# A windowed-attention and Fourier-mixing kernel: image 1 loaded ahead of the mode weights, image transposes in pairs of rows, the group norm without matmuls, and another order where there is no feed-forward and in the tail

## Chip, cores and metric

The kernel runs on one core of one Trainium2 chip. The metric is the device time of one execution in microseconds; lower is better. All data are 32-bit floats.

## What is computed

The input is 32 images of 56 x 56 tokens with 128 channels. There are two layers, each with a residual:

```python
def _gn(v, G=32, eps=1e-5):            # group norm: 32 groups of 4 channels, over the whole image
    g = v.reshape(B_, H_, W_, G, C_ // G)
    m = jnp.mean(g, axis=(1, 2, 4), keepdims=True)
    s = jnp.var(g, axis=(1, 2, 4), keepdims=True)
    return ((g - m) / jnp.sqrt(s + eps)).reshape(v.shape)
...
# layer 0: attention in windows of 7 x 7 tokens, 4 heads, image rolled by 3 in both directions
qkv = (win @ w_qkv.T).reshape(-1, N, 3, NH, hd)
attn = softmax(q @ k^T * scale + bias[rel_idx] + shift_mask)
out = (attn @ v) @ w_proj.T + b_proj   # rolled back
# layer 1: Fourier mixing along both axes, then a feed-forward
out_y = jnp.einsum('bixy,ioy->boxy', dct(x)[..., :32], w0)    # 32 modes, along the width
xy = idct(out_y padded with zeros)
...                                                           # the same along the height with w1
h = relu((xx + xy) @ W1 + b1) @ W2 + b2
# the network
x = x + layer0(_gn(x))
x = x + layer1(_gn(x))
```

## The kernel before

**Tiling.** An image is cut into 8 rows of 8 windows (a row is 7 image lines, 392 tokens). The work is a software pipeline over cycles: cycle r starts row r of all 256 (`row(cycle)` gives the image and the row; i = cycle mod 8 is the row in the image). Rows of one image are followed by those of the next without a break. The order in which TensorE (PE), ScalarE (ACT), VectorE (DVE) and GpSimd (POOL) get their instructions is written out by hand: it is the order in which the Python functions are called. Transfers are issued by the SP queue, in that order too.

**The attention of a row** goes through several cycles. In its own cycle: `attn_qk` (queries and keys, L321 and L328; VectorE writes one half of the keys, L341), `attn_v` (L353), `attn_scores` (L375, then two additions of the bias on VectorE, L383), `attn_max` (L393, and a subtraction on POOL, L394), `attn_exp` (L400). A cycle later `attn_divide` (sum L405, reciprocal L407, product on POOL, L408). Two cycles later `attn_transpose` (L419), `attn_values` (L444, evacuated to oT on ACT at L477 and on VectorE at L475), and `attn_project` (L486), whose sum with the image (L494) is written to a scratch tensor in HBM (L500). `attn_sums` (L508, L517) takes the sums for the second group norm.

**The Fourier layer of an image** starts ten cycles after its first row; c counts its cycles, so c = 0 falls on i = 2. c = 0: statistics (L528, L537) and the transform along the width (L595); c = 1, 2: that along the height, from columns loaded out of the scratch tensor; c = 3 to 5: the mode mixing (`mix`, L629), written to HBM (L639); c = 4 to 7: loaded again (`load_modes`, L650) and transformed back (`modes_back`, L668). The feed-forward of seven token groups is at c = 7, 8, 9, 10, 12, 13, 14 (`FF_AT`): `ff_in` (L711, with relu on ACT, L719; the residual is loaded at L694 and gets b2 on POOL, L701) and `ff_out` (L731, addition on VectorE L740, output DMAs L752, L753, L760). Since c goes past 8, a cycle holds the end of one image's Fourier layer and the start of the next one's. Only at c = 3 and c = 11, both on i = 5, there is no feed-forward.

**A cycle** is `full_first` (transposes, queries and keys, `load_modes`, `ff_in`, ...), then `quarters` (scores and `modes_back`), `half_columns` (`attn_v`, `transform`, `mix`), `eighths` (values), and `full_last` (`ff_out`, the next image's transposes, exponential, projection). The first ten cycles, where there is no Fourier work, are written in `first_rows`. After the last row the same functions run on with what is left of the last image.

**The next image.** `next_image` issues its load at i = 2 (L114; two buffers, so the load waits until the buffer's former image is transformed, L595) and calls `image_group` for its rows at i = 4 (2 rows), 5 (3) and 6 (3). Each call transposes four chunks of 112 tokens (two image lines each; L259), though a row is 3.5 chunks; ACT copies the row's 392 columns out of PSUM (L269), VectorE takes bn_stats (L270), POOL adds the projection's bias to the image (L274). `image_norm` is a generator, and the calls of `next(norm)` place its parts: bn_aggr (L281) at the end of i = 6; in i = 7 a matmul with the group-averaging matrix (L284), four small VectorE operations, a second such matmul (L297), the power -0.5 on POOL (L301), L303, the scaling of the qkv weights on ACT (L308) and a third matmul (L310).

**PSUM.** Four banks ("pa") rotate through all attention and image work, four ("pc") through the rest. A matmul that takes a bank waits for the readers of its last use, four allocations earlier.

**Before the cycles** the constants are loaded: image 0, small ones, the bias table (L182 adds it up on VectorE), then the mode weights w1sb and w0sb of 2 MB each and those of the feed-forward (all L125). Image 1 is loaded by `next_image` in cycle 2, so behind them in SP's queue.

## Time and profile before

| | |
|---|---|
| median of 9 runs | 3696.25 us (3694.11 to 3698.69) |
| profiled execution, its time | 3694.72 us |
| profiled execution, span from first to last instruction | 3692.9 us |
| mean granted TensorE clock | 0.997 |
| TensorE matmuls busy | 3626.5 us |
| TensorE weight loads busy | 2964.4 us |
| VectorE / ScalarE / GpSimd busy | 2183.5 / 2149.7 / 1372.3 us |
| image transposes (L259), instructions and busy | 1024, 129.9 us |
| norm matmuls L284 and L297, busy | 9.3 and 12.4 us |

A line of the timeline has the start in us from the span's start, the time from the first start to the last end of a block of equal instructions, engine, line, operation, the tiles written and read, shapes and count; in brackets stands the idle time ahead of it and what ended it. A matmul of 32-bit data is two instructions, a transpose one. Matmuls are pipelined, so that a printed block overlaps the next one. A line of the waits has the waiting instruction, what it waited for, the sum in us, how often, and the longest.

### The profile page before, as it was taken

What the parts mean: (1) busy time and instruction counts of PE and PEld (TensorE: products, weight loads), DVE (VectorE), ACT (ScalarE), POOL (GpSimd) and SP (SyncE); (2) the same over time, 40 slices, a digit from 0 to 9 for tenths busy, and PEclk for the clock granted to TensorE, in tenths of its full rate; (3) what the DMA queues carried; (4) which work ended last, traced back from release to release, by engine and by line L of the source; (5) the groups of instructions that cost most, each with busy time, mean ns of one, the idle gap of its engine ahead of it and who ended that gap; (6) DMA issues with size and microseconds to landing.
All of it is one profiled execution on the core that took longest, in us unless ns stands there. A gap on an engine that the chain in (4) does not pass through costs nothing.

```text
span 3692.9 us, 139935 instructions
## 1 busy us (share of the span) xinstructions
PE 3626.5 (98%) x61440; PEld 2964.4 (80%) x61440; DVE 2183.5 (59%) x4577; ACT 2149.7 (58%) x3915; POOL 1372.3 (37%) x1421
## 2 busy tenths in 40 slices
PE   6899999999999999999999999999999999999998
PEld 5678888888888888888888888878888888888786
DVE  6655665565666556655656665566655566565641
ACT  4555565555656555665556566556665565565653
POOL 5333343433333333434333343334333333433321
PEclk9999999999999999999999999999999999999999
DMA  4333434343434334343434343343344343443332
GB/s 112 97 99 105 114 91 111 106 112 101 113 93 116 105 103 116 92 110 105 112 101 113 95 114 107 105 113 97 105 109 109 102 113 97 111 107 105 96 107 89
DMA packets 687778, 388.93 MB, mean 105 GB/s; under 512 B 40480, under 2 KB 658113, under 8 KB 686913
## 3 DMA queue, kind: packets, MB, share of 16 engines
q1 hardware_dynamic: 686557, 379.65, 37.6%
q8 instruction: 484, 7.93, 0.9%
q14 instruction: 126, 1.02, 0.1%
q10 hardware_dynamic: 611, 0.32, 0.0%
HBM read 218.29 MB, written 161.48 MB: 103 GB/s over the span
## 4 chain that ended last, share of the span: by engine, by line
PE 93%; DVE 4%; DMA 1%; SPq 1%; ACT 1%; issue 0%; POOL 0%; ACTq 0%; POOLq 0%; DVEq 0%
PE pc L731 20%; PE pc L711 18%; PE pa L353 7%; PE pc L629 6%; PE pc L595 6%; PE pa L375 6%; PE pa L419 5%; PE pa L486 5%; PE pc L668 5%; PE pa L328 5%; PE pa L444 4%; PE pa L321 4%; PE pa L259 2%; DVE st L270 1%; DVE a L383 1%; DVE mx L393 1%
## 5 line engine op out<-in xcount | busy, mean ns | idle before, releaser
L408 POOL TENSOR_TENSOR a<-a,rs 128x784 f32<-128x784 f32 x256 | 389.9, 1523 | 1230.8 <-DVE rs L407 965.0
L731 PE MATMUL pc<-wff,hid 128*128 128x128 f32 (+1 forms) x6400 | 778.4, 279 | 0.9 <-ACT hid L719 0.7
L731 PEld LDWEIGHTS pc<-wff,hid 128*128 128x128 f32 (+1 forms) x6400 | 731.0, 189 | 21.0 <-issue 1.9
L711 PE MATMUL pc<-xf,wff 128*128 128x512 f32 (+2 forms) x1792 | 713.1, 540 | 0.4 <-ACT z L637 0.4
L719 ACT ACTIVATE hid<-pc,b1sb 128x512 f32<-128x512 f32 (+2 forms) x896 | 536.6, 635 | 97.6 <-PE pc L711 93.9
L711 PEld LDWEIGHTS pc<-xf,wff 128*128 128x128 f32 x1792 | 337.0, 190 | 301.1 <-issue 229.5
L394 POOL TENSOR_TENSOR a<-a,mx 128x784 f32<-128x784 f32 x256 | 389.5, 1522 | 451.6 <-DVE mx L393 451.2
L740 DVE TENSOR_TENSOR res<-pc,res 128x512 f32<-128x512 f32 (+2 forms) x256 | 143.6, 571 | 597.2 <-issue 273.7
L427 ACT COPY aT<-pa 113x452 f32<-113x452 f32 x256 | 137.7, 538 | 457.8 <-PE pa L419 457.7
L274 POOL TENSOR_TENSOR xl<-xl,bproj 112x384 f32<-112x384 f32 (+1 forms) x256 | 291.9, 1142 | 247.7 <-PE pa L259 243.4
L383 DVE TENSOR_TENSOR a<-pa,bm 128x392 f32<-128x392 f32 x512 | 259.5, 549 | 199.5 <-PE pa L375 199.3
L341 DVE TENSOR_SCALAR k<-pa,heads,bqkv 128x392 f32<-128x392 f32 x246 | 168.5, 685 | 275.1 <-ACT k L333 275.1
L475 DVE TENSOR_SCALAR oT<-pa,bqkv 128x98 f32<-128x98 f32 (+2 forms) x768 | 170.7, 278 | 267.7 <-PE pa L444 267.7
L400 ACT ACTIVATE a<-a 128x784 f32<-128x784 f32 x256 | 222.8, 870 | 169.9 <-POOL a L394 169.6
L360 ACT COPY v<-pa 128x512 f32<-128x512 f32 x256 | 152.6, 596 | 276.3 <-PE pa L353 276.3
L701 POOL TENSOR_TENSOR res<-res,b2sb 128x512 f32<-128x512 f32 (+2 forms) x256 | 263.6, 1036 | 100.3 <-DMA res<-scr 83.7
L375 PEld LDWEIGHTS pa<-k,q 64*64 64x64 f32 x8192 | 183.3, 132 | 137.8 <-DVE rs L407 68.2
L353 PE MATMUL pa<-wn,xw 128*64 128x128 f32 x4096 | 281.4, 280 | 3.6 <-DVE a L383 3.5
L353 PEld LDWEIGHTS pa<-wn,xw 128*64 128x64 f32 x4096 | 219.3, 137 | 51.4 <-issue 17.0
L393 DVE TENSOR_REDUCE mx<-a 128x16 f32<-128x784 f32 x256 | 247.2, 966 | 5.7
L419 PE MATMUL pa<-ident,a 113*113 113x113 f32 x2048 | 248.3, 264 | 1.6 <-POOL a L408 1.6
L405 DVE TENSOR_REDUCE sm<-a 128x16 f32<-128x784 f32 x256 | 245.7, 960 | 5.1 <-ACT a L400 5.1
(89 smaller groups left out, 5890.1 us busy)
## 6 DMA issues: line engine op xcount, KB each, us to landing
zscr<-z SPq DMA_DIRECT2D x512, 112.0 KB
htok<-scr SPq DMA_DIRECT2D x256, 196.0 KB
zT<-zscr SPq DMA_DIRECT2D x192, 256.0 KB
res<-scr SPq DMA_DIRECT2D x160, 256.0 KB
out_dram<-res SPq DMA_DIRECT2D x128, 256.0 KB
scr<-xl SPq DMA_DIRECT2D x128, 224.0 KB
xl<-in_x_dram SPq DMA_DIRECT2D x32, 784.0 KB
xl<-in_x_dram SPq DMA_DIRECT2D x32, 672.0 KB
```

Of the source, the lines that this page charges most:

```text
L274: nc.gpsimd.tensor_tensor(piece, piece, bproj.unsqueeze(1).to_broadcast([TC, n1 - n0, C]), ALU.add)
L353: nc.tensor.matmul(pv[hs, j * C : (j + 1) * C], lhsT=im.xw[i][:, w * WT : w * WT + JP], rhs=im.w[:, 2 * C : 3 * C], start=True, stop=True,)
L375: nc.tensor.matmul(ps[hp][HALVES[e], pr * 2 * WT : (pr + 1) * 2 * WT], lhsT=q[cs, w * WT : w * WT + JP], rhs=k_sb[cs, :, w], start=True, s ...
L383: nc.vector.tensor_tensor(a[:, 2 * hp : 2 * hp + 2, :, 0:WT].rearrange("p u w j -> p w u j"), ps[hp][:, :RT].rearrange("p (w u j) -> p w u ...
L393: nc.vector.tensor_reduce(mx, a3, axis=AX.X, op=ALU.max)
L394: nc.gpsimd.tensor_tensor(a3, a3, mx.unsqueeze(2).to_broadcast([P, 2 * NWR, WT]), ALU.subtract)
L408: nc.gpsimd.tensor_tensor(a3, a3, rs.unsqueeze(2).to_broadcast([P, 2 * NWR, WT]), ALU.mult)
L419: nc.tensor.transpose(pt[:PW, h * P : h * P + PW], a[:PW, h, 2 * hf : 2 * hf + 2].rearrange("p w j -> p (w j)")[:, :PW], ident[:PW, :PW],)
L701: nc.gpsimd.tensor_tensor(res[:m, c0:c1], res[:m, c0:c1], b2sb[:m].unsqueeze(1).to_broadcast([m, c1 - c0, C]), ALU.add,)
L711: nc.tensor.matmul(ph[:, :n], lhsT=wff1[:, f * P : (f + 1) * P], rhs=xff[:, t0 : t0 + n], start=True, stop=True,)
L719: nc.scalar.activation(hf[:, :n], ph[:, :n], AF.Relu, bias=b1sb[:, f : f + 1])
L731: nc.tensor.matmul(pf[:m, c * C : (c + 1) * C], lhsT=im.hid[f][:, c * P : c * P + m], rhs=wff2[:, f], start=(f == 0), stop=(f == NF - 1),)
```

## The change

1. Image 1 is loaded before the mode weights instead of in cycle 2.
2. `image_group` becomes `image_groups`: two rows at once out of seven transposes in two PSUM banks, at i = 3, 4, 5 and 6. ACT copies the first row in one piece and the second in two.
3. `image_norm` averages over the groups on VectorE: the statistics are transposed in blocks of 32, reduced over four, broadcast, and transposed back. The two matmuls with the averaging matrix go, and the whole calculation up to the power is in the first part of i = 7.
4. Cycles without a feed-forward put `half_columns` ahead of `quarters`. Before, the rule was c = 3; now it also holds for the first image's cycles c = 0, 1, 2, 4, 5, 6, where no earlier image has a feed-forward to do.
5. In the tail, after the last row's attention, the order is `half_columns`, `ff_out`, `quarters`; before it was `quarters`, `half_columns`, `ff_out`. The very last output group is added and written chunk by chunk.

```diff
--- before.py
+++ after.py
@@ -205,6 +205,8 @@
             nc.sync.dma_start(idcth[ls, : S - SS], src[:, SS:])
             nc.sync.dma_start(idcth[ls, S - SS :], src[:, :SS])
     idcth = idcth.rearrange("p h r -> p (h r)")
+    if NB > 1:
+        xls[1] = load_image(1)
     w1sb = const_load([P, NM, C], w1, "w1sb")
     w0sb = const_load([P, NM, C], w0, "w0sb")
     wff1 = const_load([P, FF], W1, "wff1")
@@ -249,63 +251,99 @@
         im.scr = dram.tile([S, S, C], F32, tag="scr", name="scr", bufs=2)
         return im
-    def image_group(im, i):
-        pt = attn_bank()
-        pt4 = pt[:, : 8 * S].rearrange("p (j r s) -> p j r s", r=8, s=WS)
-        for c in range(4):
+    def image_groups(im, i):
+        pt = [attn_bank(), attn_bank()]
+        pts = [
+            p[:, : n * S].rearrange("p (j r s) -> p j r s", r=n, s=WS) for p, n in zip(pt, (8, 6))
+        ]
+        for c in range(7):
             nc.tensor.transpose(
-                pt4[:, :, 2 * c : 2 * c + 2],
+                pts[c // 4][:, :, 2 * (c % 4) : 2 * (c % 4) + 2],
                 im.x[:, WS * i // 2 + c],
                 ident_x[:, :, SS:].rearrange("p r (j s) -> p j r s", s=WS),
             )
-        mine = pt4[:, :, i % 2 : i % 2 + WS].rearrange("p j r s -> p j (r s)")
-        im.xw[i] = big.tile([P, RT + JP - WT], F32, tag="xw", name="xw", bufs=10)
-        nc.gpsimd.memset(im.xw[i][:, RT:], 0.0)
-        xw = im.xw[i][:, :RT]
-        nc.scalar.copy(xw.rearrange("p (j t) -> p j t", t=WT), mine)
-        nc.vector.bn_stats(im.st[:, i], xw)
-        n0, n1 = WS * i // 2, WS * (i + 1) // 2
-        piece = im.x[:, n0:n1]
-        nc.gpsimd.tensor_tensor(
-            piece, piece, bproj.unsqueeze(1).to_broadcast([TC, n1 - n0, C]), ALU.add
-        )
+        for k in range(2):
+            im.xw[i + k] = big.tile([P, RT + JP - WT], F32, tag="xw", name="xw", bufs=10)
+            nc.gpsimd.memset(im.xw[i + k][:, RT:], 0.0)
+            xw = im.xw[i + k][:, :RT]
+            dst = xw.rearrange("p (j r s) -> p j r s", r=WS, s=WS)
+            if k:
+                nc.scalar.copy(dst[:, :, 0], pts[0][:, :, WS])
+                nc.scalar.copy(
+                    dst[:, :, 1:].rearrange("p j r s -> p j (r s)"),
+                    pts[1].rearrange("p j r s -> p j (r s)"),
+                )
+            else:
+                nc.scalar.copy(
+                    dst.rearrange("p j r s -> p j (r s)"),
+                    pts[0][:, :, :WS].rearrange("p j r s -> p j (r s)"),
+                )
+            nc.vector.bn_stats(im.st[:, i + k], xw)
+        n0, n1 = WS * i // 2, WS * (i + 2) // 2
+        for a, e in ((n0, n0 + 4), (n0 + 4, n1)):
+            piece = im.x[:, a:e]
+            nc.gpsimd.tensor_tensor(
+                piece, piece, bproj.unsqueeze(1).to_broadcast([TC, e - a, C]), ALU.add
+            )
+    stat = const.tile([P, C // 4], F32, tag="stat", name="stat")
+    nc.vector.memset(stat, 0.0)
     def image_norm(im):
-        mv = small.tile([P, 2], F32, tag="mv", name="mv")
-        nc.vector.bn_aggr(mv, im.st)
+        GR = C // 16
+        def average(out, src):
+            sums = small.tile([P, GR], F32, tag="gsums", name="gsums", bufs=2)
+            nc.vector.tensor_reduce(
+                sums, src.rearrange("p (g c) -> p g c", c=4), axis=AX.X, op=ALU.add
+            )
+            nc.vector.tensor_scalar(
+                out.rearrange("p (g c) -> p g c", c=4),
+                sums.unsqueeze(2).to_broadcast([P, GR, 4]),
+                0.25,
+                None,
+                ALU.mult,
+            )
         yield
-        pg = attn_bank()
-        nc.tensor.matmul(pg[:, 0:1], lhsT=gavg, rhs=mv[:, 0:1], start=True, stop=True)
-        gm = small.tile([P, 1], F32, tag="gm", name="gm")
-        nc.vector.tensor_copy(gm, pg[:, 0:1])
+        nc.vector.bn_aggr(stat[:, 0:2], im.st)
+        turned = small.tile([P, 32], F32, tag="turned", name="turned", bufs=2)
+        nc.vector.transpose(turned, stat)
+        mean = small.tile([P, 2, 32], F32, tag="gmeans", name="gmeans", bufs=2)
+        average(mean[:, 0], turned)
+        nc.vector.tensor_tensor(turned, turned, mean[:, 0], ALU.subtract)
+        nc.vector.tensor_tensor(turned, turned, turned, ALU.mult)
+        average(mean[:, 1], turned)
+        back = small.tile([P, 2, 32], F32, tag="back", name="back", bufs=2)
+        nc.vector.transpose(
+            back.rearrange("p k c -> p (k c)"), mean.rearrange("p k c -> p (k c)")
+        )
+        gm = back[:, 0, 0:1]
         nc.vector.tensor_scalar(im.xw[0][:, RT : RT + 1], gm, -1.0, None, ALU.mult)
-        d = small.tile([P, 1], F32, tag="d", name="d")
-        nc.vector.tensor_tensor(d, mv[:, 0:1], gm, ALU.subtract)
-        e = small.tile([P, 1], F32, tag="e", name="e")
+        ve = small.tile([P, 1], F32, tag="ve", name="ve")
         nc.vector.scalar_tensor_tensor(
-            out=e, in0=d, scalar=d, in1=mv[:, 1:2], op0=ALU.mult, op1=ALU.add
-        )
-        yield
-        pv = attn_bank()
-        nc.tensor.matmul(pv[:, 0:1], lhsT=gavg, rhs=e, start=True, stop=True)
-        ve = small.tile([P, 1], F32, tag="ve", name="ve")
-        nc.vector.tensor_scalar(ve, pv[:, 0:1], 1e-5, None, ALU.add)
+            out=ve, in0=back[:, 0, 1:2], scalar=1e-5, in1=back[:, 1, 0:1], op0=ALU.add, op1=ALU.add
+        )
         rstd = small.tile([P, 1], F32, tag="rstd0", name="rstd0")
         nc.gpsimd.tensor_tensor(rstd, ve, mhalf, ALU.pow)
+        im.w = work.tile([P, 3 * C], F32, tag="wn", name="wn")
+        yield
         nb = small.tile([P, 1], F32, tag="nb0", name="nb0")
         nc.vector.scalar_tensor_tensor(
             out=nb, in0=gm, scalar=-1.0, in1=rstd, op0=ALU.mult, op1=ALU.mult
         )
-        im.w = work.tile([P, 3 * C], F32, tag="wn", name="wn")
+        nc.scalar.mul(im.w, wqkv, rstd)
         yield
-        nc.scalar.mul(im.w, wqkv, rstd)
         pb = attn_bank()
         nc.tensor.matmul(pb[:, 0:1], lhsT=wqkv[:, 2 * C :], rhs=nb, start=True, stop=True)
         im.bias = small.tile([P, 5], F32, tag="bqkv", name="bqkv")
@@ -735,7 +773,10 @@
                     start=(f == 0),
                     stop=(f == NF - 1),
                 )
-        for c0, c1, m in ((0, k, P), (k, k + 1, last)):
+        parts = [(0, k, P), (k, k + 1, last)]
+        if im.b == NB - 1 and g == len(FF_GROUPS) - 1:
+            parts = [(c, c + 1, m) for c, m in enumerate(chunks)]
+        for c0, c1, m in parts:
             if m:
                 nc.vector.tensor_tensor(
                     res[:m, c0:c1],
@@ -754,7 +795,7 @@
                 c += 1
                 continue
             e = c + 1
-            while e < len(chunks) and chunks[e] == m and (o >= NT or o + (e + 1 - c) * m <= NT):
+            while len(parts) == 2 and e < len(chunks) and chunks[e] == m and (o >= NT or o + (e + 1 - c) * m <= NT):
                 e += 1
             o %= NT
             nc.sync.dma_start(
@@ -850,11 +891,15 @@
         if im:
             attn_values(im, i, cycle - 2)
-    def full_last(cycle, norm):
-        next(norm)
+    def last_out(cycle):
         for im, c in fourier(cycle):
             if c in FF_AT:
                 ff_out(im, FF_AT.index(c))
+    def full_last(cycle, norm):
+        next(norm)
+        if row(cycle - 2)[0]:
+            last_out(cycle)
         next_image(cycle)
         if row(cycle)[0]:
             attn_exp(cycle)
@@ -868,8 +913,8 @@
         if b + 1 < NB:
             if i == 2:
                 images[b + 1] = image_begin(b + 1)
-            for j in {4: (0, 1), 5: (2, 3, 4), 6: (5, 6, 7)}.get(i, ()):
-                image_group(images[b + 1], j)
+            for j in {3: (0,), 4: (2,), 5: (4,), 6: (6,)}.get(i, ()):
+                image_groups(images[b + 1], j)
@@ -912,8 +957,8 @@
     ET = mybir.EngineType
     with tc.manual_schedule(engines={ET.PE, ET.Activation, ET.DVE, ET.Pool}):
         images[0] = image_begin(0)
-        for i in range(NWR):
-            image_group(images[0], i)
+        for i in range(0, NWR, 2):
+            image_groups(images[0], i)
         for _ in image_norm(images[0]):
             pass
         norm = nothing()
@@ -922,7 +967,11 @@
                 first_rows(cycle, norm)
             else:
                 full_first(cycle, norm)
-                if (cycle - CONV_BEGIN) % NWR != 3:
+                if not row(cycle - 2)[0]:
+                    half_columns(cycle)
+                    last_out(cycle)
+                    quarters(cycle)
+                elif any(c in FF_AT for _, c in fourier(cycle)):
                     quarters(cycle)
                     if row(cycle)[0]:
                         attn_max(cycle)
```

## The prediction

> **What bounds the kernel now.** I read the page first, then TensorE's timeline in one image period, then the waits, then both ends of the run. The page:
>
> ```profile
> PE 3626.5 (98%) x61440; PEld 2964.4 (80%) x61440; DVE 2183.5 (59%) x4577; ACT 2149.7 (58%) x3915; POOL 1372.3 (37%) x1421
> PE 93%; DVE 4%; DMA 1%; SPq 1%; ACT 1%; issue 0%; POOL 0%; ACTq 0%; POOLq 0%; DVEq 0%
> ```
>
> TensorE is the only engine near full, and 93% of the chain that ended last is its own work. Its idle time before instructions, summed by place, is 30.0 us in 0 to 103 us, 17.3 in 103 to 212, only 7.6 in 212 to 3580, and 7.0 after. So in between (the L486 starts repeat every 112.76 us, one image) an instruction that leaves TensorE shortens the run, unless another engine becomes late. At the two ends waits count. A price is therefore the distance between starts, not the printed duration. Timeline of TensorE, starts first:
>
> ```profile
> 1600.32 0.98 PE L259 MATMUL pa<-ident_x,xl 112*128 112x112 f32 x8
> 1601.14 0.82 PE L486 MATMUL pa<-wproj,oT 128*112 128x128 f32 x6
> ...
> 1608.53 0.91 PE L375 MATMUL pa<-k,q 64*64 64x98 f32 x32
> 1609.37 0.81 PE L444 MATMUL pa<-aT,v 49*32 49x49 f32 x64
> 1610.11 1.50 PE L259 MATMUL pa<-ident_x,xl 112*128 112x112 f32 x12
> 1611.44 1.04 PE L486 MATMUL pa<-wproj,oT 128*112 128x128 f32 x8
> ...
> 1625.90 1.43 PE L259 MATMUL pa<-ident_x,xl 112*128 112x112 f32 x12
> 1627.18 0.82 PE L486 MATMUL pa<-wproj,oT 128*112 128x128 f32 x6
> ...
> 1629.96 0.28 PE L284 MATMUL pa<-mv,gavg 128*128 128x1 f32 x2
> 1630.10 1.97 PE L711 MATMUL pc<-xf,wff 128*128 128x256 f32 x8
> ...
> 1637.49 0.38 PE L297 MATMUL pa<-e,gavg 128*128 128x1 f32 x2
> 1637.74 2.03 PE L731 MATMUL pc<-wff,hid 128*128 128x128 f32 x16
> ```
>
> Eight image transposes take 0.82 us from start to start, twelve 1.33 and 1.28: about 0.115 each, so seven 0.70. The two matmuls of the norm take 0.14 and 0.25. In VectorE's timeline the last oT piece ahead of 1611.44 is
>
> ```profile
> 1610.43 0.66 DVE L475 TENSOR_SCALAR oT<-pa,bqkv 128x98 f32<-128x98 f32 x3
> ```
>
> It ends at 1611.09; over 25 images the L486 of this cycle (i = 5) starts 0.45 us (at least 0.34) after that end. Where TensorE does wait for oT, it starts 0.15 after. So only 0.30 can be taken out ahead of that L486.
>
> [...] the trace has 263 (median of L259), but overlapped, so the 0.115 is used. [...] L290 has 169 on average[...]. [...] L303, a one-column operation [...], has a mean of 1119 ns and in the window ended with a GpSimd addition[...].
>
> **Part 1, pairs of rows.** Per image 32 transposes become 28, and cycles i = 4, 5, 6 with 8, 12, 12 become i = 3, 4, 5, 6 with 7 each. i = 4: 0.82 to 0.70, gain 0.12. i = 6: 1.28 to 0.70, gain 0.58. i = 5: 0.63 offered, 0.30 taken, the rest a wait for oT. i = 3: loss 0.70. Sum 0.30; I take 0.25, since the second bank of i = 5 waits for the second score addition. Bounds: 0 (i = 5 gives nothing), 0.55 (no wait). ScalarE copies thrice per pair (392, 56, 336 elements), some 1.1 us against 0.9 for two rows: 0.8 more per image, at 58% busy; it costs nothing as the next user of these banks, the second L419, is some 1.3 us behind. VectorE's bn_stats and GpSimd's bias additions are as many, two rows a cycle instead of up to three. The earlier cycle needs the image earlier: SP issues its load at 1679.93 of one period, the DMA share falls from 1.18 to 0.24 at 1689, and the new L259 would start at 1698.4: 9 us to spare.
>
> **Part 2, the norm without TensorE.** Two matmuls go: 0.39 per image. Into VectorE's queue of cycle i = 7, behind the k of L341, come eleven operations: bn_aggr 0.36 (L281), seven on 32 columns at 0.19, the 64-column transpose 0.22, two one-column ones 0.31, and ten gaps of 0.03 (L286 takes 0.15, and L288, which waits for it, starts 0.19 after it): 2.5 us where 0.58 stood. Queued behind are L517, L405, L407 and the two score additions, whose banks L444 wants. From 1631.5, where L286 started, the chain ends at 1634.0, L517, L405 and L407 at 1635.6, the first addition at 1636.2; L444 needs it at 1636.6: 0.4 us is left, so nothing is lost. Bounds: 0 (the chain only grows, so no gain), and a loss of 0.6 if each transpose takes 0.7. On GpSimd the power moves ahead of L701 and L408: L701 then waits until 1634.5, and its reader L740 comes at 1640; L408 waits for L407 anyway. L303 may again meet a GpSimd subtraction, and L310 behind it has an us to spare.
>
> Parts 1 and 2: 0.64 per image, for 30 images in the full part **19 us** (bounds 10 and 28).
>
> **Part 3, image 1 ahead of the mode weights.** Five DMAs pass six. The waits before 212 us:
>
> ```profile
> PE pa L259 <- DMA xl<-in_x_dram: 9.5, 2, 7.2
> PE pa L375 <- DVE k L341: 8.1, 5, 1.8
> PE pa L486 <- DVE oT L475: 4.9, 4, 2.1
> PE pa L310 <- DVE nb L303: 4.0, 2, 2.5
> ```
>
> Of 9.5, 7.2 is image 0; 2.3 goes. SP would issue image 1 at 37.5, where w1sb was, and 8 us later it is there; L259 now wants it at about 50. The weights end some 8 us later, about 58, and are first used at 144; L500 waits behind them as before. In the norm of image 1, L284 and L310 waited 1.4 and 2.5; VectorE, which sets the pace here (it was idle 0.4 of 7.6 us in a cycle), gets 1.8 more. Together **4.5 us** (2 to 7). The norm of image 0 gets shorter too, but the first score addition (28.34) waits for the bias table, whose inputs land at 22.6: nothing.
>
> **Part 4, columns first without a feed-forward.** In the full part i = 5 alone is of that kind, and was already so ordered. It changes six of the first image's cycles. Five waits of L375 for k (1.49, 1.55, 1.84, 1.43, 1.82) are covered by L353 and the columns. The oT waits 0.57, 0.88, 0.89, 2.09 go; in their place come six of this order's own, which i = 5 shows: L444 is through at 1610.11 and oT lets L486 start at 1611.24, so 1.1 each in three cycles and 0.4 in the three that have seven transposes between. 12.6 against 4.5: **8 us** (3 if VectorE or ScalarE can't follow, 12 if the new waits are hidden). Behind the later scores are queued L393, L394 and the exponential, a cycle ahead of their user.
>
> **Part 5, the tail.**
>
> ```profile
> 3615.13 3.21 PE L668 MATMUL pc<-idcth,zT 64*64 64x112 f32 x64 [4.66 <-DMA zT<-zscr]
> ...
> 3688.44 0.69 DVE L740 TENSOR_TENSOR res<-pc,res 128x512 f32<-128x512 f32 x1 [7.02 <-PE pc L731]
> ...
> 3689.58 0.41 SPq L752 DMA_DIRECT2D out_dram<-res  x1
> 3690.04 0.36 SPq L753 DMA_DIRECT2D out_dram<-res  x1
> 3690.45 0.36 SPq L760 DMA_DIRECT2D out_dram<-res  x1
> ```
>
> L629 (1.9) and L731 (3.07) now stand ahead of this L668 and cover 4.66; the later 0.77, 0.27 and 0.20 go likewise: 5.9. SP's order is unchanged; ScalarE's z copies pass the xf copies, which helps. The last addition shrinks from 0.69 to some 0.25 [...], and one issue instead of three or four is left after it: 1.6. **7.5 us** (5 to 8).
>
> **Sum:** 19 + 4.5 + 8 + 7.5 = 39 us. The profiled execution took 3694.7 (span 3692.9), so 3655.7; the median is 1.5 above it: **3657**.
>
> **Rivals.** (a) The forecast, chance 0.66. (b) TensorE's time comes back as waits in the full part: i = 5 and 6 hang on the chain oT, L393, L394, L400, k, where L375 has 0.33 us over k in i = 6 and 0.38 in i = 7. For it: these slacks are smaller than what is taken out. Against: 0.30 and 0.14 fit in. If pairs give nothing and the ends half: 30 x 0.33 + 10 = 20, 3676 (0.27). (c) Slower: the norm's VectorE chain in i = 7. Past 2.9 us L444 waits, and past 4.2 (39/31 = 1.26 more) all is eaten. If four of the operations each meet a GpSimd one and take L303's 1.12 instead of 0.19, the chain is 6.2, the wait 3.3, 31 x 3.3 - 39 = 63: 3759. Against: GpSimd stands idle from 1630.9 to 1634.0 there, and its additions end earlier now (0.04). (d) The gains don't arrive at all, as when L259 waits for the image in i = 3: it would have to land 9 us late (0.03).
>
> **Numbers.** About 0.2%, 7 us, is what a measurement of this kernel can tell from no change. Faster is (a) and (b), 0.93; the same 0.03; slower 0.04. The low end adds the upper bounds of Parts 1, 2 and 3 (9 and 2.5) and some of Part 4: 3644. The high end reaches to (b): 3676.
>
> **What would show it.** Right: the image period falls from 112.76 to about 112.1; L486 in i = 5 starts 0.15 after oT; L668 has no idle time in the tail; L375 doesn't wait for k before 212. Wrong: TensorE idle before L444 in i = 7 (the chain), VectorE's transposes over 0.5 us, or L259 waiting on a DMA in i = 3.

## The result, and the profile after

The changed kernel takes **3675.34 us** in the median of 9 runs (3668.28 to 3675.96), beside 3697.25 for the kernel before in the same session (29 runs): a ratio of 0.9938, with a 95% interval of 0.993 to 0.9946. It is faster by 22 us. The forecast was 39 us, 3657; the measured time lies inside the range (3644 to 3676), 0.7 us below its upper end. The profiled execution took 3672.13 us (span 3670.3), 22.6 below that of before.

The page after, in the two rows shown of before: TensorE's own busy time fell by 26.6 us, and the chain of work that ended last is now TensorE for 90%, not 93%.

```profile
PE 3599.9 (98%) x61184; PEld 2934.7 (80%) x61184; DVE 2222.2 (61%) x4741; ACT 2151.6 (59%) x4043; POOL 1373.3 (37%) x1421
PE 90%; DVE 4%; ACT 2%; DMA 1%; POOL 1%; issue 1%; SPq 0%; POOLq 0%; ACTq 0%; DVEq 0%
```

To find where the 22.6 us lie, I cut both traces at two events that exist in each: the projection of row 16 (the end of the start) and the projection of row 255 (the start of the tail).

| stretch | before | after | gain | forecast |
|---|---|---|---|---|
| start, to the projection of row 16 | 216.50 | 204.80 | 11.7 | 12.5 (Parts 3 and 4) |
| full part, rows 16 to 255 | 3357.5 | 3348.4 | 9.1 | 19 (Parts 1 and 2) |
| tail, from row 255 to the end | 118.90 | 117.14 | 1.8 | 7.5 (Part 5) |

So the full part gave half of its term and the tail a quarter. The start came out as forecast, but the experiments show that its sum hides terms of other sizes.

**The full part, cycle by cycle.** The mean distance in us from projection to projection in the cycles of each i, rows 32 to 248 (the last column belongs to an experiment below):

| i | before | after | run e13 |
|---|---|---|---|
| 0 and 1 | 28.39 | 28.42 | 28.38 |
| 2 | 16.34 | **16.55** | 16.23 |
| 3 | 14.21 | 14.97 | 15.06 |
| 4 | 15.25 | 15.15 | 15.16 |
| 5 | 10.39 | 10.18 | 10.11 |
| 6 | 15.71 | 15.20 | 15.18 |
| 7 | 12.43 | 11.99 | 11.99 |
| image period | 112.72 | 112.44 | 112.11 |

In the medians, which an occasional stop doesn't move, i = 3 to 7 change by +0.72, -0.10, -0.21, -0.55 and -0.45: together -0.59, close to the -0.64 forecast. The two parts in it differ more: the pairs (i = 3 to 6) gave 0.14 where 0.25 was forecast, the norm (i = 7) 0.45 where it was 0.39. In the timeline the cycle i = 5 is now

```profile
1591.47 0.98 PE L262 MATMUL pa<-ident_x,xl 112*128 112x112 f32 x7
1592.60 1.10 PE L524 MATMUL pa<-wproj,oT 128*112 128x128 f32 x8
```

Seven transposes instead of twelve, and L524 1.13 us behind their start (1.33 before): the wait for oT stands ahead of it, as forecast (it starts 0.15 us after the last piece of oT, which ends at 1592.45). The rest of the gain is lost where the change touches nothing. TensorE's waits of the full part (440 to 3540 us; sum, times, longest):

```profile
PE pc L633 <- issue: 4.6, 6, 1.0
PE pa L413 <- DVE k L379: 2.8, 18, 0.2
PE pa L482 <- issue: 2.5, 8, 0.4
```

"Issue" means that nothing the profile shows was waited for. In the trace of before the first line had 1.5 us in 4 stops and the third 0.2 in one. All six stops at L633 stand in cycle i = 2, inside a block of transforms that depends on nothing new. One of them, with TensorE's timeline and then its busy time by the microsecond (columns: stretch, its length, PE busy, granted clock, DMA share, GB/s):

```profile
982.22 2.74 PE L633 MATMUL pc<-dct_w,xl 112*64 112x64 f32 x88
985.98 0.92 PE L633 MATMUL pc<-dct_w,xl 112*64 112x64 f32 x24 [1.03 <-issue]
```

```profile
982.00:983.00 1.00, 1.00 (x36) 1.00 1.03 206
983.00:984.00 1.00, 1.00 (x42) 1.00 0.37 80
984.00:985.00 1.00, 0.95 (x34) 1.00 0.01 1
985.00:986.00 1.00, 0.02 (x2) 1.00 0.00 0
```

And the DMA queues of the stretch 982.9 to 985.0 (packets, MB, share of 16 engines) hold one packet of another kind:

```profile
q8 instruction: 1, 0.02, 3.4%
```

That queue moves packets of 16 KB, of some 1.15 us, 482 of them beside 122368 matmuls and weight loads of TensorE in the whole run, so one for every 254; a transform block alone is 224 (112 of each). The stops at L633 come only in images in which such a packet starts 0.8 to 1.5 us behind the first transform (6 of the 15 images in which one starts 0.8 to 1.6 us behind it), and there the DMA engines are still busy: in the first and the second microsecond of the transforms the mean share is 0.94 and 0.24 in the trace of after, 0.62 and 0.06 in that of before. The busy traffic is the four transfers of the column loads (L617 before, L655 after). That these hold up TensorE's instructions is the theory that the fifth experiment tests.

**The norm.** The chain in i = 7 on VectorE, first and last operation and the one behind it:

```profile
1612.16 0.36 DVE L316 BATCH_NORM_AGGREGATE stat<-st 128x2 f32<-128x48 f32 x1
...
1614.48 0.15 DVE L334 SCALAR_TENSOR_TENSOR ve<-back 128x1 f32<-128x1 f32 x1
1614.55 0.55 DVE L555 TENSOR_REDUCE part<-sq 112x32 f32<-112x384 f32 x1
```

From 1612.16 to 1614.55 it takes 2.39 us, where 2.5 was forecast, and nothing in i = 7 waits for it.

**The tail.** TensorE and the SP queue around the first L706 (L668 before):

```profile
3585.05 8.01 SPq L677 DMA_DIRECT2D zscr<-z  x10
3593.24 0.96 SPq L688 DMA_DIRECT2D zT<-zscr  x2
3595.95 2.91 PE L706 MATMUL pc<-idcth,zT 64*64 64x112 f32 x64 [2.09 <-DMA zT<-zscr]
```

Of the 4.66 us ahead of this block 2.09 are still there: the loads of zT stand in SP's queue behind the writes of the mixing, which was moved ahead of them. Eleven writes go ahead now, eight did before, and the first load is issued 40.07 us after the projection of row 255 instead of 38.00. The later small waits changed place rather than going: 0.27, 0.42 and 0.20 now stand ahead of L749, for the xf copies of an L706 that comes directly before it; in the kernel before L629, L668 and L731 had 0.27, 0.77 and 0.20. The stop has a second price, which shows in TensorE's busy time and granted clock (columns as above):

```profile
3594.00:3596.00 2.00, 0.04 (x4) 1.00 0.83 244
3596.00:3598.00 2.00, 2.00 (x52) 0.60 0.79 233
3598.00:3600.00 2.00, 2.00 (x23) 0.55 0.64 188
```

Behind the stop the clock is at 0.50 from 3596.4 to 3599.8, and the L706 and L749 blocks take 5.2 us together; at full clock they take 3.8 (run e7 below). And the very end:

```profile
3661.99 3.17 PE L769 MATMUL pc<-wff,hid 128*128 128x128 f32 x26 [0.17 <-ACT hid L757]
3665.26 0.88 DVE L781 TENSOR_TENSOR res<-pc,res 128x128 f32<-128x128 f32 x4 [7.02 <-PE pc L769]
3665.57 0.83 SPq L801 DMA_DIRECT2D out_dram<-res  x2
...
3667.26 0.36 SPq L801 DMA_DIRECT2D out_dram<-res  x1
```

All four chunk additions come after the last matmul (3665.16), none under it, and one more transfer is issued. From the last matmul to the end it takes 5.15 us; it was 4.58.

### The profile page after: what moved, and what is told of

It reads as the page before. It is cut to its first block, busy times and chain, and to the rows that moved or that the text cites. A ratio compares the mean times of both kernels' runs of the same rounds, so it can differ in the third digit from the quotient of the medians.

```text
span 3670.3 us, 139900 instructions
## 1 busy us (share of the span) xinstructions
PE 3599.9 (98%) x61184; PEld 2934.7 (80%) x61184; DVE 2222.2 (61%) x4741; ACT 2151.6 (59%) x4043; POOL 1373.3 (37%) x1421
## 4 chain that ended last, share of the span: by engine, by line
PE 90%; DVE 4%; ACT 2%; DMA 1%; POOL 1%; issue 1%; SPq 0%; POOLq 0%; ACTq 0%; DVEq 0%
PE pc L769 20%; PE pc L749 17%; PE pa L391 7%; PE pc L633 6%; PE pc L667 6%; PE pa L413 6%; PE pa L457 5%; PE pc L706 5%; PE pa L524 5%; PE pa L482 4%; PE pa L359 4%; PE pa L366 4%; PE pa L262 2%; POOL a L432 1%; DVE a L421 1%
## 5 line engine op out<-in xcount | busy, mean ns | idle before, releaser
L749 PE MATMUL pc<-xf,wff 128*128 128x512 f32 (+2 forms) x1792 | 711.2, 539 | 0.9 <-DVE xf L717 0.6
L749 PEld LDWEIGHTS pc<-xf,wff 128*128 128x128 f32 x1792 | 339.6, 190 | 310.3 <-issue 229.1
L781 DVE TENSOR_TENSOR res<-pc,res 128x512 f32<-128x512 f32 (+3 forms) x259 | 144.1, 568 | 608.1 <-issue 293.6
L289 POOL TENSOR_TENSOR xl<-xl,bproj 112x512 f32<-112x512 f32 (+1 forms) x256 | 286.2, 1140 | 350.4 <-PE pa L262 341.9
L413 PEld LDWEIGHTS pa<-k,q 64*64 64x64 f32 x8192 | 183.8, 132 | 136.5 <-DVE rs L445 66.7
L524 PE MATMUL pa<-wproj,oT 128*112 128x128 f32 x1792 | 240.8, 274 | 14.2 <-DVE oT L513 7.2
```

Of the source, the lines that this page charges most:

```text
L289: nc.gpsimd.tensor_tensor(piece, piece, bproj.unsqueeze(1).to_broadcast([TC, e - a, C]), ALU.add)
L413: nc.tensor.matmul(ps[hp][HALVES[e], pr * 2 * WT : (pr + 1) * 2 * WT], lhsT=q[cs, w * WT : w * WT + JP], rhs=k_sb[cs, :, w], start=True, s ...
L524: nc.tensor.matmul(pp[:TC, (n - n0) * C : (n - n0 + 1) * C], lhsT=oT[:, (n - base) * TC : (n - base + 1) * TC], rhs=wproj, start=True, sto ...
L749: nc.tensor.matmul(ph[:, :n], lhsT=wff1[:, f * P : (f + 1) * P], rhs=xff[:, t0 : t0 + n], start=True, stop=True,)
```

## The experiments

All were timed beside the kernel before in the same session, and the ratios are to it, with 95% intervals. The kernel before itself took 3693.9 to 3698.9 us in these sessions, so that times of different sessions are to be compared by their ratios. "Row 16" is the time of its projection in the profiled execution (before 216.50, after 204.80).

**Each part alone, or left out.** Run e1: the kernel before with the pairs of rows alone.

```diff
-            for j in {4: (0, 1), 5: (2, 3, 4), 6: (5, 6, 7)}.get(i, ()):
-                image_group(images[b + 1], j)
+            for j in {3: (0,), 4: (2,), 5: (4,), 6: (6,)}.get(i, ()):
+                image_groups(images[b + 1], j)
```

> The kernel before with Part 1 alone (image_groups at i = 3 to 6). Theory (the cycle lengths of the changed kernel's trace add up part by part): from L486 to L486 i = 3 is 14.93, i = 4 15.15, i = 5 10.09, i = 6 15.20 instead of 14.21, 15.25, 10.30, 15.75, all others unchanged (i = 7 12.43), so 0.14 less per image, 4 us in all; with the first images about 3693. Rival (the pairs are what makes VectorE's and ScalarE's queues late): i = 0, 1, 7 grow too, and the time is 3697 or more. Second question, the stops before L595 and L444 at i = 2 that nothing in the profile explains (6 us in the steady part after, 3 before): if the pairs bring them, i = 2 has 16.5 on average; if not, 16.3.

3702.75 us, ratio 1.0018 (1.0009 to 1.0026): slower than before. The image period is 112.69, so the full part gains next to nothing; i = 3 to 6 have the medians of the changed kernel. What is lost is lost in the start: row 16 at 227.5, 11 us late. Image 1 is now wanted at i = 3 and comes behind the weights; the wait for it is 10.9 us. The pairs need the early load.

Run e2: the kernel before with the new `image_norm` alone.

> The kernel before with Part 2 alone (norm on VectorE). Theory: i = 7 is 11.98 instead of 12.43, nothing else moves: 0.45 x 30 = 13.5 us less, and some 1 us from the waits before L284 and L310 in the norm of image 1: about 3682. Rival (the chain in VectorE's queue costs what the matmuls gave): i = 7 stays over 12.3 because L444 waits, 3695. The first norm: the chain runs beside GpSimd's bias additions, so it should again take some 5 us instead of 2.4, and L310 not come before 20 us.

3691.18 us, ratio 0.9993 (0.9985 to 1.0002): not told from before. The cycle i = 7 falls from 12.43 to 11.98 as it should, but i = 2 rises to 16.58, with 5.5 us of stops in 8 places ahead of the width transforms. So the stops come with the norm's edit, in a cycle that it doesn't touch.

Run e3: the changed kernel without Part 4.

```diff
-                elif any(c in FF_AT for _, c in fourier(cycle)):
+                elif (cycle - CONV_BEGIN) % NWR != 3:
```

> The changed kernel without Part 4 (scores first again wherever c is not 3). Theory: only the six cycles of the first image between 97 and 190 us change; the waits of L413 for k come back, the project of row 16 starts 8 us later than 204.8, and the time is 8 us longer, 3683. Rival (the first rows are bound by VectorE whatever the order): 2 us or less, 3676.

3675.69 us, ratio 0.9952 (0.994 to 0.9965). Row 16 at 210.33: 5.5 us later in the trace; the two ratios to before don't tell it from the changed kernel. TensorE's waits before row 16 in this run

```profile
PE pa L413 <- DVE k L379: 8.7, 5, 2.3
PE pa L524 <- DVE oT L513: 3.6, 3, 1.6
```

and in the changed kernel (up to 205 us):

```profile
PE pa L524 <- DVE oT L513: 6.2, 4, 2.3
PE pa L391 <- ACT aT L465: 2.4, 4, 0.7
PE pa L413 <- DVE k L379: 0.8, 1, 0.8
```

The k waits go as forecast, 7.9 us; 2.6 of them come back as waits for oT, 2.4 as waits for aT, which the prediction did not have, and 0.8 as stops without a releaser. A wait of 1.0 for the scaled weights, which only this run has, goes too. That leaves 3.1 us in waits. The other 2.4 us aren't Part 4's: TensorE's granted clock was at 0.50 from 77.6 to 87.9 us in this profile, ahead of the first cycle that the edit changes, and from 77.3 to 80.7 in the changed kernel's. Run e7, where it was low from 77.2 to 87.4, has row 16 at 207.21, 3.1 us ahead of this run.

Run e4: the changed kernel without Part 3.

```diff
-    if NB > 1:
-        xls[1] = load_image(1)
```

> The changed kernel without Part 3 (image 1 loaded in cycle 2 again, behind the mode weights). Theory: L262 is wanted at 48.8 now and the image is there at 58, so it waits 9 us instead of the 2.3 of before, and the loss is about 8 us, not the 2.3 of my sum: 3683. Rival (VectorE catches up behind the wait, since it sets the pace): 2 to 4 us, 3678.

3685.06 us, ratio 0.9972 (0.9964 to 0.998). Row 16 at 216.65, 11.9 us later: the whole gain of the start is gone, with Part 4 still in. The profile shows why it is so dear. TensorE's timeline, and then its busy time and granted clock (third number from the right):

```profile
57.29 1.54 PE L260 MATMUL pa<-ident_x,xl 112*128 112x112 f32 x7 [9.46 <-DMA xl<-in_x_dram]
58.63 1.54 PE L357 MATMUL pa<-xw,wn 128*128 128x392 f32 x2
```

```profile
48.00:50.00 2.00, 0.00 (x0) 1.00 0.88 290
50.00:52.00 2.00, 0.00 (x0) 0.93 0.86 233
52.00:54.00 2.00, 0.00 (x0) 0.50 1.15 249
...
58.00:60.00 2.00, 2.00 (x8) 0.50 0.50 129
60.00:62.00 2.00, 2.00 (x7) 0.51 0.00 0
62.00:64.00 2.00, 2.00 (x42) 1.00 0.01 4
```

The wait is 9.5 us; 4 us into it the granted clock falls to 0.50, and it comes back 4.7 us after work has resumed. The seven transposes take 1.34 us to the next block; in the changed kernel's full part they take 0.72. This stop of TensorE thus cost twice: 9.5 us of idle time, and 4.7 us of work at a clock of 0.50.

**The stops at i = 2.** Run e5: the changed kernel with the two column loads of c = 0 (four transfers) issued late, from ScalarE's queue.

```diff
-                load_columns(im, 0)
-                load_columns(im, 1)
...
+        for im, c in fourier(cycle):
+            if c == 0:
+                load_columns(im, 0, nc.scalar)
+                load_columns(im, 1, nc.scalar)
...
```

> The changed kernel, except that the two column loads of a pass (eight transfers, L617/L655) are issued from ScalarE's queue after its exponential at the end of the cycle, not from SyncE's ahead of the cycle's work. Theory A (the stops at i=2 ahead of L633's transforms are TensorE waiting for its own instructions, whose fetch meets the eight column transfers in the DMA engines): the mean of the i=2 cycle falls from 16.55 us to about 16.25, the idle time before L633 for which the profile names no releaser falls from 4.63 us in 6 stops to under 1.5, and 5 to 9 us go over 29 images: about 3668. Rival B (the stops come with the place in the program, not with the column transfers): the stops stay at 4 to 7 us and the time is within 3 us of the changed kernel's, about 3675. Rival C (the columns now land too late): idle time appears before the half-column matmuls that end on L617's transfers, some 0.3 us or more in each image, 3684 or more.

(The transfers are four, not eight.) 3699.74 us, ratio 1.0007 (0.9999 to 1.0015). Both A and C came true. The i = 2 cycle is 16.25, and of the six packets of instructions that start 0.8 to 1.6 us behind the first transform none brings a stop at L633; the DMA share is 0.02 there. But i = 3 grows from 14.97 to 15.90, because the columns are late (waits of 440 to 3560 us):

```profile
PE pc L633 <- DMA htok<-scr: 11.1, 17, 1.4
```

Run e10 puts the same four transfers 2 us earlier, behind the third and fourth transform (the two calls at the start of the cycle go, as in e5).

```diff
                 for g in range(4):
                     transform(im, True, g)
+                    if g > 1:
+                        load_columns(im, g - 2, nc.scalar)
```

> The changed kernel, with the four transfers of the two column loads (L617/L655) issued from ScalarE's queue behind its copies of the third and fourth transform at i=2, some 3 and 4 us after the transforms start: behind the stretch in which a late fetch of instructions stops TensorE, and 1 to 2 us ahead of where the run with late columns had them. Theory A (the stops are the fetch against these transfers): mean i=2 cycle 16.25 us (16.55 now) and no idle time ahead of L633 without a releaser; the i=3 cycle at 14.95 to 15.1 us since the columns come in time; 4 to 8 us below the changed kernel, about 3669. Rival B (the columns are again late, since the loads of the image after next, issued 3.5 to 4.7 us after the transforms start, share the DMA engines): the i=3 cycle stays above 15.5 us and the time is 3690 or more.

3673.41 us, ratio 0.9937 (0.9922 to 0.9952): not told from the changed kernel. In the trace i = 2 is 16.25 and L633 has no stop; i = 3 is 15.23 in the mean (median 14.92), since some columns are still late. So the stops go, but a gain in time isn't shown. Its profiled execution was the slowest of its six (3686.23), and its row 16 is at 215.96; the granted clock was at 0.50 for 27 us of this start, which the last experiment takes up.

**Two pairs at i = 5.** Run e6.

```diff
-            for j in {3: (0,), 4: (2,), 5: (4,), 6: (6,)}.get(i, ()):
+            for j in {4: (0,), 5: (2, 4), 6: (6,)}.get(i, ()):
```

> The changed kernel, with the pairs put at i=4, 5, 5, 6 in place of 3, 4, 5, 6. Theory A (i=5 ends on a wait for oT, so that the seven transposes of a pair are nearly free there, while at i=3 they cost what they take): i=3 goes from 14.93 back to 14.21 us, i=5 from 10.09 to about 10.45, a net -0.36 us per image, 10 us in all: about 3665. Rival B (the second pair's banks and ScalarE copies make the exponentials late): the i=5 or i=6 cycle grows by 0.7 us or more, with waits of L413 or L524 in the profile, and the time is the changed kernel's or up to 5 us above it, 3675 to 3680.

3676.10 us, ratio 0.9941 (0.9929 to 0.9954). i = 3 falls by 0.69, but i = 5 rises by 0.43, i = 6 by 0.21 and i = 2 by 0.08: the period is 112.51. The new wait is none of those that I named: L366, the query and key matmuls, finds its bank not yet read by VectorE's sum of the projection.

```profile
PE pa L366 <- DVE xl L532: 8.1, 23, 0.4
```

**The tail.** Run e7: the last image's zscr writes from ScalarE's queue.

```diff
-            nc.sync.dma_start(
+            (nc.scalar if im.b == NB - 1 else nc.sync).dma_start(
```

> The changed kernel, with the last image's eleven writes of a column chunk (L639/L677) issued from ScalarE's queue, so that the loads of zT stand in SyncE's queue ahead of nothing that is late. Theory A (L706's 2.09 us wait at 3595.95 is zT's load issued late, at 3593.24, behind these writes): that wait goes to under 0.3 us, and the tail from 117.14 to about 115; 2 us, 3673. Rival B (zT's loads wait for the writes of the chunks themselves, wherever these are issued): the wait stays at 2 us and the time is that of the changed kernel, 3675.

3673.13 us, ratio 0.994 (0.9927 to 0.9953); medians can't tell 2 us. In the trace the tail is 114.87, 2.3 shorter, and L706 waits no more:

```profile
3594.86 0.91 SPq L688 DMA_DIRECT2D zT<-zscr  x2
...
3598.74 1.69 PEld L706 LDWEIGHTS pc<-idcth,zT 64*64 64x64 f32 x64 [0.17 <-issue]
```

Counted from row 255, the load is issued 1.7 us earlier (38.4 against 40.1). It isn't all gained: ScalarE, which now issues the writes, makes L749 and L667 wait 0.68 and 0.55 before. So L706 starts only 0.5 us earlier; 1.5 more come from the clock, which stays at 1.00 behind it, and 0.3 at the very end. A holds for the wait, and its size is right by this other sum.

Run e8: a PSUM bank for each chunk of the last group.

```diff
-        pf = conv_bank()
+        final = im.b == NB - 1 and g == len(FF_GROUPS) - 1
+        pfs = [conv_bank() for _ in chunks] if final else [conv_bank()] * len(chunks)
...
```

> The changed kernel, with a PSUM bank of its own for each chunk of the last feed-forward group (instead of one bank for all of them), so that each VectorE addition waits for its own chunk's matmuls alone. Theory A (the split of the end brought nothing because the first addition waits for the bank's last matmul): the first additions and writes run under the last chunk's matmuls, and from TensorE's last matmul to the end it takes 3.4 to 3.6 us instead of 5.15: -1.6 us. Rival B (the end is the last chunk's own addition, issue and transfer, whatever went before): 4.6 to 5.1 us, 0 to -0.5 us.

3670.77 us, ratio 0.9931 (0.9919 to 0.9943). The additions now run under the matmuls, and only the last comes after:

```profile
3664.33 0.29 DVE L782 TENSOR_TENSOR res<-pc,res 128x128 f32<-128x128 f32 x1 [4.34 <-PE pc L770]
3664.65 1.18 SPq L802 DMA_DIRECT2D out_dram<-res  x2
...
3666.95 0.29 DVE L782 TENSOR_TENSOR res<-pc,res 128x128 f32<-128x128 f32 x1 [0.60 <-PE pc L770]
3667.27 0.36 SPq L802 DMA_DIRECT2D out_dram<-res  x1
```

From the last matmul (3666.92) to the end it takes 3.33 us instead of 5.15: 1.8 gained. A holds. What made the split useless was the shared bank.

**Image 1 early, alone.** Run e11: the kernel before with the two lines of Part 3.

> The kernel before, with image 1 loaded ahead of the mode weights and nothing else of the change. Theory A (the prediction's: only the 2.3 us that L259 waited for image 1, and some of the 3.9 us of its norm's waits, can go): row 16 is projected at 212 to 214.5 us instead of 216.5, and the time is 2 to 4.5 us below that of before, 3691 to 3694. Rival B (the early load is worth what it was worth beside the pairs, where leaving it out cost 11.9 us): row 16 at 205 to 207, 3686. Rival C (the waits of the old norm and the stops of VectorE take up what goes): row 16 at 215 to 217, no difference.

3692.44 us (22 runs), ratio 0.9982 (0.9976 to 0.9988). Row 16 at 211.75, 4.75 us earlier: nearest to theory A, though up to 2.4 of it can be the clock, which was low for 4.8 us less than before. The same edit is worth 11.9 beside the pairs.

**Together.** Run e12: e10, e7 and e8 in one.

> The changed kernel with three edits together: the column loads from ScalarE's queue behind the third and fourth transform, the last image's chunk writes from ScalarE's queue, and a PSUM bank for each chunk of the last group. If they add up, the tail (last projection to end) is 117.14 - 2.3 - 1.8 = 113 us, the i=2 cycle 16.25 us on the mean, and the time 4 + (0 to 8) us below the changed kernel's, 3664 to 3671. If the columns are late again, the i=3 cycle shows it and the time is about 3690. If the two edits of the tail overlap (both end on the same chain), the tail is 115 us.

3672.69 us, ratio 0.9932 (0.992 to 0.9945), a little above what I expected. The tail is 113.49, near the 113.0 of the sum, but not because its two edits add up: e10 alone, with neither, already has 114.52. One issue of SP's queue ahead of the zT load takes 0.62 us there and 1.58 in the changed kernel, L706 waits 1.26 instead of 2.09, and the clock doesn't fall. So the move of the columns and that of the writes shorten the same stop. The period is 112.24. But in image 0 the later columns cost 3.8 us, in a start where nothing covers them.

Run e13: e12 with image 0's columns at their old place, and eleven matmuls in TensorE's two idle stretches of the norm of image 1, whose result nobody reads.

```diff
+        if cycle == NWR - 1:
+            filler(7)
         if im:
             attn_scores(im, i, cycle)
...
             attn_v(im, i, cycle)
+        if cycle == NWR - 1:
+            filler(4)
```

> The run with three edits, where image 0's columns are loaded at their old place (its columns came 3.8 us late in the start, L633), and where eleven matmuls whose result nobody reads (wff1 on itself, 128 columns) fill TensorE's two idle stretches in the norm of image 1, seven ahead of L413 (2.2 us idle) and four ahead of L348 (1.3 us idle). Theory A (TensorE's granted clock falls to 0.50 after such idle stretches and the work behind them runs at half speed until it has been busy for some us; that, and not the idle time alone, makes the start so dear and so uneven): the clock stays at 1.00 between 74 and 90 us, row 5 is projected some 10.5 us after row 4 (12.7 where the clock fell, 11.1 where it hardly did), the L633 wait for htok before 160 us is gone, row 16 comes at 201 to 204 us and the time is 3664 to 3668. Rival B (the clock falls for another reason, such as the waits of 0.3 to 0.5 us in each cycle): it shows 0.5 to 0.65 between 80 and 90 us nevertheless, and only the 3.8 us of the columns go, 3669. Rival C (the filler delays L413 and L348 by as much as it saves): row 5 at 12 us or more after row 4 with the clock at 1.00.

**3665.49 us** (3661.05 to 3666.96), ratio 0.9921 (0.9908 to 0.9935): the lowest median of all, 28 us below before, though the intervals of e12 and e13 overlap. The filler's work is seen in the clock. In run e7, whose code in this stretch is that of the changed kernel (columns as above):

```profile
74.00:76.00 2.00, 0.15 (x4) 1.00 0.00 0
76.00:78.00 2.00, 1.65 (x92) 0.80 0.32 83
78.00:80.00 2.00, 1.74 (x32) 0.50 0.04 11
...
84.00:86.00 2.00, 2.00 (x8) 0.50 0.00 0
86.00:88.00 2.00, 2.00 (x16) 0.64 0.00 0
```

and with the filler:

```profile
74.00:76.00 2.00, 2.00 (x22) 1.00 0.00 0
76.00:78.00 2.00, 1.36 (x17) 1.00 0.04 8
78.00:80.00 2.00, 1.52 (x92) 1.00 0.33 86
...
84.00:86.00 2.00, 2.00 (x15) 1.00 0.00 0
```

The clock stays at 1.00, where it fell between 77 and 81 us in all eight other profiles with these two idle stretches. B falls. Row 5 follows row 4 after 11.1 us: 1.6 less than where the clock was low for 6.8 to 10.2 us (12.7 in e3, e4, e7, e8 and e10), but no less than where it was low for 3.4 (11.1 in the changed kernel, e5 and e12). The 10.5 expected is not reached, and a gain in time by the filler alone is not shown. The wait for htok is gone; row 16 comes at 204.46, half a microsecond past the expected stretch. The full part, rows 16 to 255, takes 3340.7: 16.8 us less than before, where the forecast for Parts 1 and 2 was 19.

## Why the prediction was right or wrong

**Right: that it is faster, and what it does to TensorE's cycles.** Seven transposes for 0.72, the oT wait that takes 0.4 of the 0.6 us that i = 5 offers (0.3 was forecast), the norm's chain of 2.39 us that nothing waits for: i = 3 to 7 gave 0.59 per image, 0.64 was forecast. Rival (c), the slow chain, did not occur: VectorE's transposes took 0.21 and 0.25 us. The prices of its operations, 0.19 for 32 columns and 0.22 for the transpose of 64, were not shown by the trace of before; in the trace of after the medians are 0.18 to 0.21 and 0.25. The last addition of 128 columns, put at some 0.25, took 0.29 in e8. Of the four signs of being right one came as stated, L524 0.15 us after oT. The period fell to 112.44 and not to 112.1, L706 still waits in the tail, and L413 waited once for VectorE's k in the start, for 0.8 us.

**Wrong: "Parts 1 and 2: 0.64 per image, for 30 images 19 us".** The sum took it that a microsecond of TensorE's work removed stays removed unless another engine becomes late. Of 0.59 only 0.28 arrived; 0.21 was lost in i = 2, the rest in small waits of other cycles. Rival (b) gave 3676, which is the measured time, but its mechanism, L413 waiting for k, is only 2.8 us in the full part: that the time lies inside the range, whose upper end (b) had set, is luck. What happened, as far as the runs show, is that packets of the instruction queue (by their number TensorE's own) meet the column loads. Two runs with the loads elsewhere (e5, e10) had i = 2 at 16.25 and no stop, and e13, with that and the rest, has the period of 112.1 that the prediction asked for. (e10 and e12, with the same code in the full part, have 112.48 and 112.24; the five profiles with the changed kernel's full part have 112.37 to 112.45.)

Why the change made the stops more frequent is half open: e2 shows that the norm's edit is enough. A packet comes at another place against the transforms from image to image, and the edit changes the number of TensorE's instructions in between (61440 matmuls before, 61184 after); and the DMA engines are busier in that moment than before. Both show in the traces. With the new norm and the columns at their old place (seven runs) a packet starts 0.8 to 1.6 us behind the first transform in 13 to 18 of 27 images, and the DMA share of the first microsecond is 0.94 to 0.98; with the old norm (three runs) it is 7 or 8 images and 0.62 to 0.65. A stop at L633 comes in 37 of these 103 images with the new norm and in 2 of the 23 with the old one. With the columns moved (four runs) the share is 0.02, and 22 such packets bring no stop. So the packet alone isn't enough; why the norm's edit raises the share stays open.

**Wrong in its terms: the start.** Part 3 was put at 4.5 us; alone it is 4.75 (partly by the clock, so the agreement is in part luck), but with the pairs it is 11.9, because the pairs want image 1 a cycle earlier and the prediction compared only with the wait of the kernel before. Part 4 was put at 8 and is 5.5 in the trace, of which 3.1 in waits: the k waits went, but the oT waits grew and the aT waits were missing from its sum; the rest goes with a lower clock ahead of Part 4's cycles (e3 against e7). Both differences contain something that I left out altogether, the granted clock. Between 43 us and row 16 it was at 0.50 for 15.1 us before, 6.8 after, 13.7 in e3 and 20.5 in e4. By my estimate half of each, 7.5, 3.4, 6.8 and 10.2 us, is the most that the clock cost: at 0.50 the seven transposes of e4 took 1.34 us instead of 0.72, and TensorE isn't always what the others wait for. So of Part 3's 11.9 us 6.8 could be clock, and of the whole start's 11.7 4.1. The low stretches ahead of the run's end last 3.41 us or two to four times that (4.7 us of work passed in e4 until the third of them had ended), and the moment varies: the same code had 0.97 between 80 and 90 us in the changed kernel's profile and 0.63 in e7's. What makes the clock fall is not settled by the traces. It fell behind stops of 2.2 us in the start and 2.09 in the tail, and in the 3.41 us ahead of the fall at 77.25 TensorE had been busy for 1.21; behind a stop of 2.89 us from 99.91, in the same profile, it stayed at 1.00. That the moment varies is also why one profiled start is no measure to better than 2 or 3 us: e7 and e8, whose start is the changed kernel's, have row 16 at 207.2 and 207.1.

**Wrong: "SP's order is unchanged" in the tail.** That queue isn't written by hand in the way the four engines are: with the mixing moved ahead, three more of its writes (eleven instead of eight) went ahead of the zT loads, which left 2.07 us later. So "cover 4.66" became 2.57, and e7's trace confirmed it by moving the writes. "The later 0.77, 0.27 and 0.20 go likewise" failed, as each moved on to L749. The tail's clock was left out too: behind L668's stop of 4.66 us in the kernel before it was at 0.50 for 3.41 us, and behind the 2.09 us that stayed it is so again, so that nothing of this came back. And "1.6" for the split of the last addition was a loss of 0.57: I counted the operations left after the last chunk but not what the first waits for, which is the last matmul into its bank (e8). The two repairs of e12 give a tail of 113.5, where 111.4 was forecast.

## What to carry to other kernels

When work is moved, ask for each moved transfer which queue it stands in and what then stands behind it; and when an evacuation is cut into pieces, ask whether each piece has a bank of its own. An idle stretch of TensorE ahead of dense work cost more than its own length here where the granted clock fell behind it, to 0.50 for 3.4 to 10.2 us (by my estimate up to half of that), so a start should be priced with the granted clock beside the waits. Stops that the profile puts down to nothing are worth setting against the instruction queue's packets and the DMA share at that moment, and a term that is right in the medians of its cycles can still be lost in another cycle.

## What the runs showed of the hardware

- TensorE stopped for up to 1.4 us at a time (e6) where a packet of 16 KB on the instruction queue started 0.8 to 1.6 us behind the first transform and the DMA engines had been busy in the first microsecond (mean share 0.94 to 0.98): in 37 of 103 such images. Moving four transfers by about 7 us (e10) or 9 us (e5) removed these stops. That TensorE lacked its instructions is inferred from the packets.
- The granted clock fell to 0.50 behind idle stretches of 1.9 us (e8, tail), 2.1 and 2.2 us (the changed kernel, tail and start), and in one of 9.5 us (e4), for multiples of 3.41 us; behind one of 2.89 us (the changed kernel, from 99.91) it stayed at 1.00, and so it did in the one profile of e13, with eleven matmuls whose result nobody reads in the idle stretches.
- The first image's norm, which runs beside GpSimd's additions, takes 5.0 us instead of 2.4; two of its operations, of 32 columns each, took 0.93 and 1.28 us where 0.19 is usual:

```profile
15.86 0.93 DVE L322 TENSOR_TENSOR turned<-turned,gmeans 128x32 f32<-128x32 f32 x1
16.82 1.28 DVE L323 TENSOR_TENSOR turned<-turned 128x32 f32<-128x32 f32 x1
```

  GpSimd's additions run without a break from 14.53 to 19.00. The first operation ends at 16.79, where a pair of them has just ended (16.74), the second at 18.10, where the next one has (18.05). In the other 31 images, where no GpSimd instruction runs beside them, the two take 0.19. The trace of before has the same at L303, of one column: 0.16 us in the three images in which GpSimd is idle beside it, 1.21 to 1.22 in the other 29, where it ends 0.01 to 0.02 us behind a GpSimd addition (L701). Why these operations last so long isn't shown. The prediction had such meetings in rival (c) for i = 7, where GpSimd stands idle (for 4.73 us up to 1614.71), and not for image 0. L348 starts at 20.70, where L310 started at 20.08, but the start doesn't pay for it: the first score addition, which waits for the bias table as the prediction said, comes at 28.22 (28.34 before).
